# A two-layer graph network on one core: finishing the last row tile bank by bank, with an early test and a branch hint

## The chip, the cores and the metric

The kernel runs on one NeuronCore of a Trainium2 chip. The metric is the device time of one execution in microseconds (us), the median of several runs; smaller is better. A core has five engines that run their own instruction streams and wait for one another by semaphores: PE (TensorE, matrix products, with a separate row PEld for its weight loads), DVE (VectorE), ACT (ScalarE), POOL (GpSimd) and SP (SyncE, which issues DMAs here). Products land in PSUM[...].

A profile is one execution recorded by the hardware. Its span runs from the first to the last instruction and is a little shorter than the measured time.

## The reference, cut to what matters

Two layers, each with a layer norm, a ReLU and a residual. The first attends within graphs of rows; the second is a graph attention over an adjacency matrix of 4096 by 4096 with eight heads of 64 columns.

```python
h = jnp.maximum(_layernorm(x, axis=-1), 0.0)
x = x + _L0_gnn_ref(h, adj, adj, ptr, Wq, bq, Wk, bk, Wv, bv)
h = jnp.maximum(_layernorm(x, axis=-1), 0.0)
x = x + _L1_gnn_ref(h, adj, W, a_origin, a_dst)

def _L1_gnn_ref(x, adj, W, a_origin, a_dst):
    mx = jnp.einsum('nf,hfd->hnd', x, W)
    s_i = jnp.einsum('hnd,hd->hn', mx, a_origin)
    t_j = jnp.einsum('hnd,hd->hn', mx, a_dst)
    logits = s_i[:, :, None] + t_j[:, None, :]
    masked = jnp.where(adj[None] > 0, logits, neg_inf)
    attn = jax.nn.softmax(masked, axis=-1)
    out_h = jnp.einsum('hij,hjd->hid', attn, mx)
    return jnp.transpose(out_h, (1, 0, 2)).reshape(N, H * D)
```

In the softmax of the second layer s_i is constant along a row and drops out. So each row's result is a sum over its neighbours of exp(t_j) times mx_j, divided by the sum of exp(t_j): a product of the 0/1 mask with a matrix of 512 weighted columns and eight columns of weights, and a division.

## The kernel before

The kernel has a straight path, fully unrolled, which holds where the graphs are the row tiles and all sums stay within bounds, and a general path behind a branch, which recomputes everything and is skipped when the bounds hold. It is skipped with the inputs measured here.

The last stage of the straight path, the aggregation, goes over 32 row tiles of 128 rows. Each weighted column is kept as a high and a low part, so a tile is 3 groups (CB) of 174 columns (CW1), each with its low parts behind it: 348 columns a matmul. The last group ends with the sums of weights (columns 512 to 519).

```python
def aggregate(sb, ps_g, i, part):
    mw = sb.tile([P, P // B, N // BY // (P // B)], F32, name="mw", bufs=1)
    ...                                             # four DMAs of the packed mask, a transpose
    at = sb.tile([P, NT, P], F32R, name="at")
    nc.vector.tensor_copy(...)                      # L277: mask bytes to fp32r
    pg = ps_g.tile([P, CB, 512], F32, name="pg")    # three banks
    for j in range(NT):
        for c in range(CB):
            nc.tensor.matmul(                       # L283
                pg[:, c, : 2 * CW1], at[:, j, :],
                part(j)[:, c].rearrange("p s w -> p (s w)"),
                start=(j == 0), stop=(j == NT - 1),
            )
    tot = sb.tile([P, EW], F32, name="tot")
    tot3 = tot.rearrange("p (c w) -> p c w", c=CB)
    nc.scalar.copy(tot3, pg[:, :, :CW1])            # L290
    nc.vector.tensor_tensor(tot3, tot3, pg[:, :, CW1 : 2 * CW1], ALU.add)   # L291
    return tot
```

The loop over the tiles, and the test behind it:

```python
ps_g = straight.enter_context(tc.tile_pool(name="ps_g3", bufs=2, space=PSUM))
...
for i in range(NT):
    row = sb3.tile([P, D], F32, name="row3", bufs=1)
    nc.sync.dma_start(row, x1_d[i])
    tot = aggregate(sb3, ps_g, i, lambda j: parts[j])
    if i + 1 < NT:
        nc.gpsimd.tensor_copy(den_all[:, i : i + 1], tot[:, ES : ES + 1])
    else:
        nc.vector.tensor_scalar(held[:, 5:6], tot[:, ES : ES + 1], 0.0, None, ALU.is_gt)   # L597
    r = small.tile([P, H], F32, name="r")
    nc.vector.tensor_scalar(r, tot[:, ES:EC], 1e-30, None, ALU.max)     # L599
    nc.vector.reciprocal(r, r)                                          # L600
    num = tot[:, :D]
    if i + 1 < NT:
        scaled(num, r)                                                  # L296
        nc.gpsimd.tensor_add(num, num, row)                             # L604
        nc.scalar.dma_start(out[ts(i, P), :], num)
    else:
        for g in range(2):
            half = ts(g, HW)
            scaled(num[:, half], r[:, ts(g, H // 2)])
            nc.vector.tensor_add(num[:, half], num[:, half], row[:, half])   # L610
            nc.scalar.dma_start(out[ts(i, P), half], num[:, half])           # L611
    ...                                             # bounds of earlier stages into held
with tc.tile_pool(name="ps_ok", bufs=1, space=PSUM) as ps:
    all_held = small.tile([P, 1], F32, name="all_held")
    nc.vector.tensor_reduce(all_held, held, AX.X, ALU.min)              # L623
    pt = ps.tile([P, P], F32, name="pt_ok")
    nc.tensor.transpose(pt[:1, :], all_held, ident)                     # L625
    least = small.tile([1, 1], F32, name="least")
    nc.vector.tensor_reduce(least, pt[:1, :], AX.X, ALU.min)            # L627
    nc.vector.tensor_scalar(bad_i, least, 1.0, None, ALU.is_lt)         # L628
bad = nc.values_load(bad_i[0:1, 0:1], min_val=0, max_val=1)             # L629: each engine reads it

with tc.If(bad > 0):                                                    # L632
    ...                                             # the general path, some 270 lines
```

Instructions, semaphores and buffers are ordered and placed by the compiler from the data dependencies; the order on one engine can differ from the program's.

## Time and profile before

| what | value |
|---|---|
| time, median of 3 runs | 974.26 us (972.87 to 974.94) |
| span of the profile | 970.5 us, granted clock 0.992 |
| PE busy | 940.3 us, 97% of the span |
| aggregation matmuls (L283) | 3072, busy 489.6 us |
| DVE busy | 459.4 us, 47% |
| ACT busy | 260.7 us, 27% |
| instruction packets | 41 on queue 8, 31 on queue 14 |

In the profile a line such as "L283 PE MATMUL pg<-part,at ..." names the program's line, the engine, the operation and the tiles written and read. The first number after the bar is the time in which at least one of them ran, the second the mean length of one in ns. The chain of waits is followed back from the last computing instruction, so what comes after that one isn't in it. An engine name with a q is that engine's sequencer, which handles loads of registers, branches and semaphores; these do not count as busy. Instruction packets are the DMA transfers that bring program code to the engines.

### The profile page before, as it was taken

To read this page: it belongs to the slowest core of one execution; us is meant where nothing else is said; L and a number is where in the kernel's file an instruction comes from. 1 tells how busy PE (TensorE), PEld (TensorE's weight loads), DVE (VectorE), ACT (ScalarE), POOL (GpSimd) and SP (SyncE) were. 2 spreads that over 40 slices of the span, in tenths; PEclk is the share of its full clock that TensorE was granted. 3 is DMA by queue.
4 is the path that set the end of the run, shared out by engine and by line. 5 is a ranking of instruction groups with operands and counts; after the bars stand their busy time and mean duration, and the time that the engine had idled before them with its cause. 6 is when DMAs were issued, how large, how long until landed. Compare 5 with 4: busy or idle time off the path is not lost.

```text
span 970.5 us, 13180 instructions
## 1 busy us (share of the span) xinstructions
PE 940.3 (97%) x5051; PEld 817.5 (84%) x5051; DVE 459.4 (47%) x978; ACT 260.7 (27%) x505; POOL 184.0 (19%) x344
## 2 busy tenths in 40 slices
PE   8999999989999998999999999999999999999995
PEld 5676677766677776788999999999999999999994
DVE  4678777866766358655133242433424233242321
ACT  5865666665762222233100000000000000000000
POOL 2211113231122125555110110101011010110100
PEclk9999999999999999999999999999999999999998
DMA  9989889898883033221022312223131221312201
GB/s 343 419 346 378 322 329 364 355 369 317 336 339 148 33 104 108 72 66 55 1 76 56 88 50 82 62 69 87 44 87 52 80 85 47 87 49 82 61 27 37
DMA packets 58042, 148.28 MB, mean 153 GB/s; under 512 B 6386, under 2 KB 23026, under 8 KB 49778
## 3 DMA queue, kind: packets, MB, share of 16 engines
q1 hardware_dynamic: 48178, 130.31, 38.3%
q10 hardware_dynamic: 9792, 17.05, 4.6%
q8 instruction: 41, 0.67, 0.3%
q14 instruction: 31, 0.25, 0.1%
HBM read 113.77 MB, written 33.55 MB: 152 GB/s over the span
## 4 chain that ended last, share of the span: by engine, by line
PE 89%; DVE 3%; DMA 2%; POOL 2%; ACT 2%; issue 1%; SPq 0%; ACTq 0%; DVEq 0%; POOLq 0%
PE pg L283 50%; PE pp L420 11%; PE pp L408 10%; PE pp L243 9%; PE pp L493 3%; PE pss L466 3%; PE pt L127 2%; DMA row<-x_d 1%; POOL part L231 1%; DMA xg<-x 1%; DVE a L136 1%; ACT junk L443 1%; DVE row L121 0%; DVE stats L114 0%; POOL rstd L120 0%
## 5 line engine op out<-in xcount | busy, mean ns | idle before, releaser
L283 PE MATMUL pg<-part,at 128*128 128x348 f32 x3072 | 489.6, 321 | 1.2 <-DVE e L252 1.2
L283 PEld LDWEIGHTS pg<-part,at 128*128 128x128 f32 x3072 | 489.4, 188 | 1.5 <-issue 1.5
L277 DVE CAST at<-at 128x4096 fp32r<-128x4096 fp8e4 x32 | 74.0, 2313 | 312.2 <-PE pg L283 312.2
L290 ACT COPY tot<-pg 128x522 f32<-128x522 f32 x32 | 19.2, 599 | 470.5 <-PE pg L283 470.5
L443 ACT ACTIVATE junk<-a 128x2048 bf16<-128x2048 f32 (+15 forms) x92 | 124.4, 1352 | 48.7 <-DVE x L495 28.0
L243 PE MATMUL pp<-w1x,hT 128*128 128x256 f32 (+1 forms) x512 | 118.4, 385 | 0.0
L420 PE MATMUL pp<-wv,hT 128*128 128x512 f32 x256 | 116.6, 600 | 0.0
L408 PE MATMUL pp<-hT,m_sb 128*128 128x256 f32 x512 | 113.2, 379 | 0.0
L243 PEld LDWEIGHTS pp<-w1x,hT 128*128 128x128 f32 x512 | 95.7, 192 | 13.6
L408 PEld LDWEIGHTS pp<-hT,m_sb 128*128 128x128 f32 x512 | 96.1, 190 | 12.9 <-issue 0.5
L420 PEld LDWEIGHTS pp<-wv,hT 128*128 128x128 f32 x256 | 49.1, 192 | 61.9 <-issue 61.9
L136 DVE TENSOR_SCALAR a<-a 128x512 fp8e4<-128x512 f32 x256 | 98.2, 460 | 0.5 <-DMA a_d<-a 0.4
L595 POOL COPY den_all<-tot 128x1 f32<-128x1 f32 x31 | 5.8, 186 | 369.1 <-DVE tot L291 369.1
L128 ACT ACTIVATE hT<-pt 128x512 f32<-128x512 f32 x64 | 37.0, 598 | 68.8 <-PE pt L127 68.7
L604 POOL TENSOR_TENSOR tot<-tot,row 128x512 f32<-128x512 f32 x31 | 40.0, 1290 | 61.7 <-DVE tot L296 61.7
L231 POOL TENSOR_TENSOR part<-e,part 128x522 fp32r<-128x522 f32 x32 | 42.1, 1316 | 43.0 <-ACT part L230 38.8
L118 POOL TENSOR_SCALAR ve<-mv 128x1 f32<-128x1 f32 x64 | 18.7, 295 | 150.9 <-DVE mv L116 150.8
L252 DVE TENSOR_TENSOR e<-pp,e 128x256 f32<-128x256 f32 x64 | 26.6, 417 | 28.9 <-ACT e L371 25.2
L270 DVE STREAM_TRANSPOSE at<-mw 128x1024 f32<-128x1024 f32 x32 | 39.5, 1236 | 0.0
L120 POOL TENSOR_TENSOR rstd<-ve,neghalf 128x1 f32<-128x1 f32 x64 | 38.5, 604 | 4.4
L424 DVE TENSOR_TENSOR v<-pp,bv_sb 128x512 f32<-128x512 f32 x32 | 22.0, 688 | 36.0 <-PE pp L420 36.0
L412 ACT ACTIVATE gT<-pp,c_sb 128x256 f32<-128x256 f32 x64 | 29.7, 468 | 29.4 <-PE pp L408 29.3
(93 smaller groups left out, 584.1 us busy)
## 6 DMA issues: line engine op xcount, KB each, us to landing
a<-adj SPq DMA_DIRECT2D x64, 1024.0 KB, 13.1
a_d<-a SPq DMA_DIRECT2D x32, 512.0 KB, 10.6
row<-x_d SPq DMA_DIRECT2D x64, 256.0 KB, 3.5
mw<-a_d SPq DMA_DIRECT2D x128, 128.0 KB, 4.0
xg<-x SPq DMA_DIRECT2D x16, 512.0 KB, 4.7
x_d<-x ACTq DMA_DIRECT2D x32, 256.0 KB, 4.2
out<-tot ACTq DMA_DIRECT2D x31, 256.0 KB, 3.8
wkT_sb<-wkT SPq DMA_DIRECT2D x4, 256.0 KB, 6.3
```

The source lines that it names most:

```text
L120: nc.gpsimd.tensor_tensor(rstd, ve, neghalf, ALU.pow)
L128: nc.scalar.activation(dst, pt, AF.Relu)
L136: nc.vector.tensor_scalar(a8v[:, u], av[:, u], 0.0, None, ALU.is_gt, saturate=False)
L231: nc.gpsimd.tensor_sub(dst[:, :, 1, :], e3, dst[:, :, 0, :].bitcast(F32))
L243: nc.tensor.matmul(pm[g][:, :n], hT[:, k, :], w1x[:, k, g * HW : g * HW + n], start=(k == 0), stop=(k == KC - 1),)
L270: nc.vector.transpose(at8.rearrange("p c n b -> p (c n b)").bitcast(F32).rearrange("p (c u n) -> p c u n", c=NW, n=B), mw.rearrange("p u ( ...
L277: nc.vector.tensor_copy(at.rearrange("p (c b) q -> p c b q", b=BY), at8.rearrange("p c q b -> p c b q"))
L283: nc.tensor.matmul(pg[:, c, : 2 * CW1], at[:, j, :], part(j)[:, c].rearrange("p s w -> p (s w)"), start=(j == 0), stop=(j == NT - 1),)
L408: nc.tensor.matmul(pp[:, : G * P], m_sb[:, k, ts(m, P)], hT[:, k, :], start=(k == 0), stop=(k == KC - 1),)
L420: nc.tensor.matmul(pp, hT[:, k, ts(t, P)], wv[:, k, :], start=(k == 0), stop=(k == KC - 1))
L443: nc.scalar.activation(junk[:, c0:c1], a[:, c0:c1], AF.Exp, scale=2.0 * NEG, accum_out=sums[:, n : n + 1],)
L604: nc.gpsimd.tensor_add(num, num, row)
```

## The change

The first 31 tiles are aggregated as before. The last one is finished bank by bank. Its matmuls run group after group in place of alternating: first the last group, which holds the sums of weights, then columns 0 to 173, then 174 to 347. Each group is evacuated, scaled, added to the residual and stored by itself while PE works on the next, so that only the last group's work lies behind the last matmul. The reciprocals of the sums are spread to 512 columns once, as `rb`. The test of the bounds is made from the first group's sums: the minimum over rows is transposed on PE between the second and the third group, so that the flag is known early. Ahead of the last tile a branch hint is placed on all five engines, which tells them that the jump over the general path is likely.

```diff
-    def aggregate(sb, ps_g, i, part):
+    def load_mask(sb, i):
...
+        return at
+
+    def product(pg, at, part, j, c):
+
+        nc.tensor.matmul(
+            pg[:, : 2 * CW1], at[:, j, :], part(j)[:, c].rearrange("p s w -> p (s w)"),
+            start=(j == 0), stop=(j == NT - 1),
+        )
...
-        for i in range(NT):
+        for i in range(NT - 1):
...                                  # the loop's body, without its cases for the last tile
+        tc.mark_branch_hint_location("general", "LikelyTaken", tuple(getattr(mybir.EngineType, e) for e in ("PE", "DVE", "Activation", "Pool", "SP")))
+        i = NT - 1
+        row = sb3.tile([P, D], F32, name="row3", bufs=1)
+        nc.sync.dma_start(row, x1_d[i])
+        at = load_mask(sb3, i)
+        ps_l = straight.enter_context(tc.tile_pool(name="ps_l3", bufs=2, space=PSUM))
+        tot = sb3.tile([P, EW], F32, name="tot")
+        rb = sb3.tile([P, EW], F32, name="tot")
+        for c in (CB - 1, 0, 1):
+            if c == 1:
+                pg = ps_g.tile([P, CB, 512], F32, name="pg")[:, 0]
+            else:
+                pg = ps_l.tile([P, 512], F32, name="pl")
+            for j in range(NT):
+                product(pg, at, lambda j: parts[j], j, c)
+            part = tot[:, ts(c, CW1)]
+            nc.scalar.copy(part, pg[:, :CW1])
+            nc.vector.tensor_tensor(part, part, pg[:, CW1 : 2 * CW1], ALU.add)
+            if c == CB - 1:
+                r = heads_rest(tot)
+                nc.vector.tensor_scalar(held[:, 5:6], tot[:, ES : ES + 1], 0.0, None, ALU.is_gt)
+                all_held = small.tile([P, 1], F32, name="all_held")
+                nc.vector.tensor_reduce(all_held, held, AX.X, ALU.min)
+                nc.vector.tensor_copy(
+                    rb[:, :D].rearrange("p (h d) -> p h d", d=HD),
+                    r[:, :, None].to_broadcast([P, H, HD]),
+                )
+            if c == 0:
+                pt = ps_g.tile([P, CB, 512], F32, name="pg")[:, 0, :P]
+                nc.tensor.transpose(pt[:1, :], all_held, ident)
+                least = small.tile([1, 1], F32, name="least")
+                nc.vector.tensor_reduce(least, pt[:1, :], AX.X, ALU.min)
+                nc.vector.tensor_scalar(bad_i, least, 1.0, None, ALU.is_lt)
+            here = slice(c * CW1, min((c + 1) * CW1, D))
+            nc.vector.tensor_tensor(tot[:, here], tot[:, here], rb[:, here], ALU.mult)
+            nc.vector.tensor_tensor(tot[:, here], tot[:, here], row[:, here], ALU.add)
+            nc.scalar.dma_start(out[ts(i, P), here], tot[:, here])
     bad = nc.values_load(bad_i[0:1, 0:1], min_val=0, max_val=1)

-    with tc.If(bad > 0):
+    with tc.If(bad > 0, label="general"):
```

## The prediction

> **What bounds the kernel now.** I read the page's chain first: 50% of the span is the aggregation matmul and 89% is TensorE. The change leaves all those matmuls in place, so whatever it brings must come from after the last of them. The chain of waits over the last 12 us, then:

> ```profile
> 955.97 2.40 PE pg L283 x15
> 958.37 0.02 issue
> 958.40 0.60 ACT tot L290
> 959.00 0.02 issue
> 959.02 0.71 DVE tot L291
> ...
> 960.60 0.42 DVE tot L296
> 961.02 0.67 DVE tot L610 x2
> 961.69 0.20 DVE least L627
> 961.89 0.02 issue
> 961.91 0.14 DVE bad_i L628
> ```

> Columns are start, length and what ran. TensorE is done at 958.37, and 3.7 us of a serial tail follow: evacuation of three banks, their sum, scaling, residual, the test. But the chain stops at 962.06 and the span at 970.5. The windows view of what lies between (columns: length, busy PE, PEld, DVE, ACT, POOL, clock, DMA share, GB/s):

> ```profile
> 958.40:962.10 3.70, 0.27 (x1) 0.08 (x1) 2.93 (x11) 0.59 (x1) 0.00 (x0) 1.00 0.00 0
> 962.10:962.80 0.70, 0.00 (x0) 0.00 (x0) 0.00 (x0) 0.00 (x0) 0.00 (x0) 0.72 0.62 212
> 962.80:966.10 3.30, 0.00 (x0) 0.00 (x0) 0.00 (x0) 0.00 (x0) 0.00 (x0) 0.50 0.17 49
> ```

> From 962.1 on no engine computes anything; that is 8.4 us, over twice the tail. The instructions of the branch's line, by engine, tell why:

> ```profile
> L632 DVEq EVENT_SEMAPHORE  x2: 21/21/21, 966.1 to 966.2; - x2
> L632 ACTq EVENT_SEMAPHORE  x2: 17/17/17, 966.2 to 966.2; - x2
> L632 PEldq EVENT_SEMAPHORE  x2: 51/51/51, 967.1 to 967.3; - x2
> ...
> L632 DVEq COMPARE_BRANCH  x1: 76/76/76, 962.7 to 962.7; - x1
> L632 PEldq COMPARE_BRANCH  x1: 4322/4322/4322, 962.8 to 962.8; - x1
> L632 ACTq COMPARE_BRANCH  x1: 54/54/54, 962.8 to 962.8; - x1
> ```

> Every engine branches at 962.7 to 963.0, and the next instruction of DVE and ACT comes at 966.1 to 966.2, 3.3 us later; PE's branch itself lasts 4.32 us. The DMA view of 963.6 to 964.6 holds these packets and nothing else:

> ```profile
> q14 instruction: 4, 0.03, 12.8%
> q8 instruction: 1, 0.02, 12.1%
> ```

> Five instruction fetches, one for each engine: the jump goes to code that isn't there yet. A second hole follows. Of the closing line's waits SyncE does three by 967.38 and the next at 969.33, though all they wait for had happened by 967.35 (PE's second semaphore above). Another four 8 KB instruction packets moved at 966.7 to 966.9, so I take that for a second fetch[...]: 1.9 us. The end is then 1.15 us of remaining waits and barrier.

> [...]

> **The change, part by part.**

> *Order of matmuls.* 96 matmuls of 348 columns stay 96, each with its own weight load before and after. The tile now takes 15.30 us (943.1 to 958.4), 159 ns each. Banks are now filled in 32 matmuls, 5.10 us: sums at 948.2, columns 0 to 173 at 953.3, columns 174 to 347 at 958.4. Does accumulating into one bank without rotation slow a matmul? The projections already do so four in a row at 216 ns for 256 columns, no sign of a stall. I assume 159 ns unchanged. The transpose for the test now lies between the second and the third bank: one slot at the 109 ns at which the kernel's other transposes follow one another. Last matmul: 958.36 + 0.11 = 958.47.

> *First two banks and the test.* After the first bank: copy, add, maximum and reciprocal, test, minimum, and a 512-wide copy of the reciprocals, some 2.5 us from 948.2. The copy writes the buffer of the tile before, whose store was issued at 947.24 and lands in 3.8 us, at 951.0; so the scaled sums are out by about 952.5. all_held is ready by 951.7, before the transpose at 953.3. least and bad_i end at about 954.1. Nothing of this delays PE.

> *The third bank, serial.* Lengths from the trace at two sizes. ACT copies: 256 columns 364 ns, 522 columns 599, so 174 columns 364 - 82 x 0.883 = 0.29 us. DVE: 256 columns 420, 512 columns 692, so 174 columns 0.33. Handovers 0.03 each.
> 958.47 + 0.04 + 0.29 (copy) + 0.03 + 0.33 (add) + 0.03 + 0.33 (scale) + 0.03 + 0.33 (residual) + 0.03 = 959.91, issue of the last store, where it was 961.82. It lands 1.7 us later (the median of the two half stores): 961.6, was 963.5. Gain to here: 1.9 us.

> *The flag is early.* PE, POOL and SP have nothing after the flag but their own work: SP and POOL can read it at 954.2 (0.57 us) and branch at 954.9; PE branches after its last matmul, about 958.6. Even unhinted, their fetches end at 958.2 and 962.9. DVE reads it at 959.9 and branches at 960.6. ACT reads it after its last store issue (0.36): 960.3 + 0.47 + 0.1 = 960.9.

> *The hint.* It is put ahead of the last tile, some 15 us before the branch; the fetch needs 3.3. If it works, ACT goes on at about 961.2 in place of 960.9 + 3.3 = 964.2. I take 0.3 us for a hinted jump, a guess of a few branch lengths (50 to 76 ns); no run shows it yet. SyncE's second fetch is hidden with or without the hint, since SyncE then sits at the target from 958.2 at the latest, and its next block (3.0 us after arrival in this trace, 966.3 to 969.3) is there by 961.2.

> *Sum.* What ends last is SyncE, waiting for the last store at 961.6. Then eight resets (0.6; the store's semaphore, next in rotation, is probably an early one in its list), nine closing waits at 0.07 (0.63), drains (0.13), and the barrier as now, 969.73 to 970.47 (0.74): 963.7. The span falls from 970.5 to 963.7, by 6.8 us, 1.9 of it from the shorter tail, 3.0 from the jump, 1.9 from SyncE's second fetch. On the 974.26 us measured: 967.5.

> **The rivals.**
> *The hint does nothing, or is lost.* [...] Then ACT and DVE are the last: ACT at 964.2, two resets and a drain 0.25, SyncE's last waits 0.35, drains and barrier 0.87: 965.7. Gain 4.8, time 969.5. I give this 25%.
> *Nothing in the tail counts, the stores' landing ends the kernel anyway.* The trace speaks against: the last store's packets end at 963.4, 7 us before the end.
> *Single-bank accumulation is slower.* At 10 ns more for each of 96 matmuls it takes back 1.0 us: 968.5. The 216 ns row speaks against it; it could as well be a little faster[...].
> *A wait takes its place.* The order on an engine isn't the program's: at 927.81 DVE casts the mask of the last tile before it adds tile 29's banks at 930.02, though the program has two tiles' work between. The hint stands ahead of the last tile's mask in the program. If nothing may pass it, the cast (2.29 us) falls behind tile 30's add, 944.5, and PE, which is through with tile 30 at 943.1, waits some 3.7 us: 971.4. If on the contrary the hint floats far ahead[...]: 970 and more. Likewise a transpose moved behind the third bank makes the flag 0.7 us late and opens all five fetches again: 970. I give these together 15%. The banks speak for no wait: six for the rotating pair, two for the new pool, all long free.
> [...]

> **Range and chances.** 967.5 is the sum with a working hint; the rivals nearly all lie above it, up to 972, and pull the middle to 967.9. The runs of before themselves spread by 2.1 us. Eight times in ten: 965.0 to 971.5. Two per cent would be 19.5 us, more than all that follows the last matmul (12.1), so faster by over 2% is about 1%; slower by over 2% needs a stall no part here explains, 1%.

> **What would show it.** Right: the last store issued near 959.9; compare-branches of SP and POOL before 956 and of ACT near 961; ACT's next instruction within 0.5 us of its branch, with its instruction packets near 944 and none after the branch; no hole in SyncE's closing waits; span near 963.7. Wrong: 3.3 us after ACT's or DVE's branch (hint lost), a last matmul later than 959 (accumulation, transpose, or a cast held back by the hint), a bad_i after the last matmul (order).

## The result, and the profile after

| | before | after |
|---|---|---|
| time, median of 6 runs each | 973.04 us (972.23 to 974.94) | 966.17 us (962.86 to 967.85) |
| ratio after to before | | 0.9924, 95% interval 0.9906 to 0.9942 |
| span of the profile | 970.5 us | 961.1 us |
| last aggregation matmul ends at | 958.36 | 955.31 |
| from there to the end of the span, "tail" below | 12.11 us | 5.76 us |

The two profiles' spans differ by 9.4 us, the medians by 6.9. Some 3.1 us of the 9.4 are not the change's: the aggregation starts at 468.7 us in the profile before and at 465.6 in the one after, and over all profiles at 465.6 to 470.1, whatever the kernel. From there to its last matmul it takes 489.6 us before and 489.7 after, the slot of the transpose. All else that the change brings lies behind the last matmul, so the tail is what is compared from here on. It fell by 6.35 us, or 6.25 less the slot.

The chain of waits of the changed kernel from the last tile on (start, length, what ran):

```profile
939.93 10.20 PE pl L284 x64
950.13 0.11 PE pg L655
950.24 5.09 PE pg L284 x32
955.33 0.02 issue
955.35 0.31 ACT tot L642
955.66 0.02 issue
955.69 0.35 DVE tot L643
956.03 0.02 issue
956.06 0.35 DVE tot L660
956.41 0.02 issue
956.43 0.34 DVE tot L661
```

The first two groups of the last tile take 10.20 us for 64 matmuls, the third 5.09 for 32: 159 ns each, as with alternating banks. The transpose takes a slot of 0.11 us. Behind the last matmul four short operations are left, 1.46 us, where 3.7 us of them stood before. The windows view of the tail (length, busy PE, PEld, DVE, ACT, POOL, clock, DMA share, GB/s), cut at the issue of the last store and at its landing:

```profile
955.31:956.80 1.49, 0.00 (x1) 0.00 (x0) 1.02 (x3) 0.30 (x1) 0.00 (x0) 1.00 0.00 0
956.80:959.18 2.38, 0.00 (x0) 0.00 (x0) 0.00 (x0) 0.00 (x0) 0.00 (x0) 0.96 0.15 44
959.18:961.10 1.92, 0.00 (x0) 0.00 (x0) 0.00 (x0) 0.00 (x0) 0.00 (x0) 0.50 0.00 0
```

So the tail is now 1.5 us of work, 2.4 us of a store that lands, 1.9 us of closing waits and barrier. The branch's line, by the sequencer of each engine (count, then shortest, median and longest in ns, then the first and last start):

```profile
L666 SPq EVENT_SEMAPHORE  x9: 17/17/17, 952.3 to 959.7; - x9
...
L666 PEldq EVENT_SEMAPHORE  x2: 51/51/51, 955.4 to 955.6; - x2
L666 DVEq EVENT_SEMAPHORE  x2: 21/21/21, 957.7 to 957.8; - x2
L666 ACTq EVENT_SEMAPHORE  x2: 17/17/17, 958.2 to 958.3; - x2
L666 POOLq COMPARE_BRANCH  x1: 65/65/65, 951.5 to 951.5; - x1
L666 SPq COMPARE_BRANCH  x1: 70/70/70, 951.8 to 951.8; - x1
L666 PEldq COMPARE_BRANCH  x1: 408/408/408, 952.9 to 952.9; - x1
L666 DVEq COMPARE_BRANCH  x1: 89/89/89, 957.1 to 957.1; - x1
L666 ACTq COMPARE_BRANCH  x1: 68/68/68, 957.7 to 957.7; - x1
```

PE's branch lasts 408 ns where it lasted 4322, DVE and ACT go on about 0.5 us after theirs where it was 3.3. SyncE branches 3.5 us before the last matmul ends, does its first reset at 952.3 and then waits for the store until 959.18. Where the hint itself stands is the surprise. The closing line of the program, to which the compiler books it:

```profile
L939 POOLq BRANCH_PREFETCH_HINT  x1: 48/48/48, 0.7 to 0.7; - x1
...
L939 PEldq BRANCH_PREFETCH_HINT  x1: 50/50/50, 0.8 to 0.8; - x1
```

It was written ahead of the last tile, but stands at the head of all five streams, some 950 us before the branch. That it depends on no other instruction, so that the compiler could move it there, is my reading.

### The profile page after: what moved, and what is told of

It reads as the page before. It is cut to its first block, busy times and chain, and to the rows that moved or that the text cites. A ratio compares the mean times of both kernels' runs of the same rounds, so it can differ in the third digit from the quotient of the medians. Undisturbed runs are those within 1.5% of the kernel's fastest.

```text
span 961.1 us, 13194 instructions
## 1 busy us (share of the span) xinstructions
PE 937.3 (98%) x5051; PEld 817.2 (85%) x5051; DVE 460.7 (48%) x983; ACT 260.7 (27%) x507; POOL 185.0 (19%) x344
## 4 chain that ended last, share of the span: by engine, by line
PE 89%; DVE 4%; DMA 2%; POOL 2%; ACT 2%; issue 1%; SPq 0%; ACTq 0%; DVEq 0%; POOLq 0%
PE pg L284 50%; PE pp L428 11%; PE pp L416 10%; PE pp L243 9%; PE pp L501 3%; PE pss L474 3%; PE pt L127 2%; DMA row<-x_d 1%; PE pl L284 1%; POOL part L231 1%; DMA xg<-x 1%; DVE a L136 1%; DVE row L121 1%; ACT junk L451 1%; POOL rstd L120 0%
## 5 line engine op out<-in xcount | busy, mean ns | idle before, releaser
L284 PE MATMUL pg<-part,at 128*128 128x348 f32 x3008 | 479.6, 322 | 1.2 <-DVE e L252 1.2
L284 PEld LDWEIGHTS pg<-part,at 128*128 128x128 f32 x3008 | 479.1, 188 | 1.6 <-issue 1.5
L416 PEld LDWEIGHTS pp<-hT,m_sb 128*128 128x128 f32 x512 | 96.2, 190 | 12.8 <-issue 0.5
```

Source lines behind the costliest of these rows:

```text
L284: nc.tensor.matmul(pg[:, : 2 * CW1], at[:, j, :], part(j)[:, c].rearrange("p s w -> p (s w)"), start=(j == 0), stop=(j == NT - 1),)
L416: nc.tensor.matmul(pp[:, : G * P], m_sb[:, k, ts(m, P)], hT[:, k, :], start=(k == 0), stop=(k == KC - 1),)
```

## The experiments

All tails in one table; the sections follow. "Landing" is from the issue of the last store to its last semaphore update; all numbers are us.

| kernel | tail | jump of ACT | landing | hole in SyncE's waits |
|---|---|---|---|---|
| before | 12.11 | 3.31 | 1.76 | 1.9 |
| after (three profiles) | 5.76, 5.75, 5.79 | 0.42 | 2.37, 2.36, 2.39 | none |
| before with the hint | 7.16 | 0.42 | 1.77 | none |
| after without the hint | 6.58 | 2.89 | 2.46 | 0.4, before ACT arrives |
| after, test behind the third bank | 6.56 | 0.42 | 3.17 | none |
| after, hint on DVE and ACT alone | 6.08 | 0.42 | 2.69 | none |
| before, one spare load on SyncE | 11.85 | 3.16 | 1.77 | 1.7 |
| before, hint on POOL alone | 10.09 | 3.14 | 1.77 | none |
| after, two more DVE products at the end | 6.01 | 0.42 | 2.61 | none |
| after, order 2, 1, 0, three stores | 5.13 | 0.42 | 1.73 | none |
| after, order 2, 1, 0, two stores | 4.48, 4.48 | 0.42 | 1.60, 1.60 | none |

### The changed kernel again

No edit.

> The changed kernel once more, for how far its end repeats. Tail means the time from the end of the last aggregation matmul to the end of the span: 12.1 us before, 5.8 us after. Theory: the tail is a fixed chain and repeats within 0.2 us; the last store lands 2.4 us after its issue because its rows are 696 B. Rival: the 2.4 us (1.7 for the half stores of before) were chance; then the store lands in 1.7 us and the tail is about 5.1 us.

Measured: tail 5.75 us, landing 2.36. The tail repeats to a few hundredths (a third profile, further down: 5.79), and the long landing is no chance. So single profiles of a variant can be compared by their tails, though their times can't to that accuracy.

### The hint alone

```diff
         for i in range(NT):
+            if i + 1 == NT:
+                tc.mark_branch_hint_location("general", "LikelyTaken", ...)   # all five engines
             row = sb3.tile([P, D], F32, name="row3", bufs=1)
...
-    with tc.If(bad > 0):
+    with tc.If(bad > 0, label="general"):
```

> The kernel before with the hint alone. Theory (a hint given at any distance works, the compiler puts it at the program's start, some 960 us ahead): every engine's next instruction 0.4 to 0.5 us after its branch in place of 3.3, PE's branch 0.4 in place of 4.3, no instruction packets between the branches and the first instruction at the target; SyncE's second fetch (3.0 us from its arrival) stays, since nothing else has become earlier: tail 12.1 - 2.9 = 9.2 us, time about 3 us less than before. Rival (the hint is lost over 960 us, the short jump of the changed kernel comes from something else): tail 12.1 us, time as before.

Measured: tail 7.16 us, 967.28 us, ratio to before 0.9952 (0.9924 to 0.998). The branch's line of this kernel:

```profile
L634 SPq EVENT_SEMAPHORE  x9: 17/17/17, 963.5 to 964.1; - x9
...
L634 ACTq EVENT_SEMAPHORE  x2: 17/17/17, 963.3 to 963.3; - x2
L634 DVEq EVENT_SEMAPHORE  x2: 21/21/21, 963.3 to 963.4; - x2
...
L634 PEldq COMPARE_BRANCH  x1: 408/408/408, 962.7 to 962.7; - x1
L634 ACTq COMPARE_BRANCH  x1: 68/68/68, 962.8 to 962.8; - x1
L634 SPq COMPARE_BRANCH  x1: 70/70/70, 963.0 to 963.0; - x1
```

The branches come at the same times as before, and all engines go on 0.4 to 0.5 us later in place of 3.3. The hint works from the head of the program; the rival falls. But the tail is 2.0 us shorter than the theory said: SyncE's second stall is gone too, which I had not expected of the hint. Instruction packets still move at 963.8 to 964.1, but SyncE goes through its waits (964.2 to 965.4 with the barrier) without stopping for one. It gets its own test further down. The one line of the hint alone is thus worth 4.95 of the change's 6.35 us.

### The change without the hint

```diff
-        tc.mark_branch_hint_location("general", "LikelyTaken", ...)
```

> The changed kernel without the hint. Theory (the hint spares the fetch at each jump, but only the engines that branch last, DVE and ACT, are on the path): 3.3 us behind each branch, SP's, POOL's and PE's of it hidden under the third bank's matmuls; ACT goes on 6 us after the last matmul, tail 7.2 us, 1.5 us more than with the hint. Rival A (the early flag alone makes all jumps harmless): tail 5.8 us. Rival B (the hint is worth a whole fetch, 3.3 us): tail 9 us.

Measured: tail 6.58 us, 966.68 us, ratio 0.9952 (0.9924 to 0.9979). The branch's line:

```profile
L665 SPq EVENT_SEMAPHORE  x9: 17/17/17, 956.8 to 962.3; - x9
...
L665 PEldq EVENT_SEMAPHORE  x2: 51/51/51, 958.9 to 959.0; - x2
L665 DVEq EVENT_SEMAPHORE  x2: 21/21/21, 962.4 to 962.5; - x2
L665 ACTq EVENT_SEMAPHORE  x2: 17/17/17, 963.1 to 963.2; - x2
...
L665 PEldq COMPARE_BRANCH  x1: 3442/3442/3442, 955.4 to 955.4; - x1
L665 DVEq COMPARE_BRANCH  x1: 76/76/76, 959.5 to 959.5; - x1
L665 ACTq COMPARE_BRANCH  x1: 54/54/54, 960.2 to 960.2; - x1
```

The last matmul of this profile ends at 957.78. Every engine stands behind its jump again, 2.5 to 3.0 us and 3.44 in PE's branch, but SyncE and PE go on at 956.8 and 958.9, and DVE and ACT alone (962.4 and 963.1) behind the store's landing (961.7). ACT's jump took 2.89 us, not 3.3, which is 0.4 of the 0.6 us by which the tail is below what was expected. SyncE has a short hole in its closing waits, 0.4 us (962.60 to 962.96) where it was 1.9, and had reached the target nearly 6 us before; it then waits for ACT until 963.27, which sets the end. Both rivals fall: the early flag doesn't make the jumps harmless, and the hint is not worth a whole jump's 3.3 us on top of it. It is worth 0.8 us.

### The test behind the third bank

```diff
-            if c == 0:
+            if c == 1:
                 pt = ps_g.tile([P, CB, 512], F32, name="pg")[:, 0, :P]
```

> The changed kernel with the test of the bounds behind the third bank, as before, and with the hint. Theory (the early flag is worth SyncE's second fetch, which needs 3.0 us from its arrival at the target): SyncE arrives some 3.4 us after the last matmul, has its next block at 6.4, tail about 7.5 us. Rival (with the hint the early flag is worth nothing, since the last store's landing ends last): tail about 5.9 us.

Measured: tail 6.56 us, 966.84 us. The number lies between the two and the reason is neither. SyncE reaches the target 2.15 us after the last matmul, earlier than I had reckoned, and has no hole. What is longer is the last store:

```profile
L662 ACTq DMA_DIRECT2D out<-tot x3: 339/339/339, 951.7 to 959.2; - x3
...
DMA to landing us min/median/max: 1.6/1.7/3.2
```

The store of the second bank now lands in 1.6 us (2.1 to 2.6 in the profiles with the early test), the last one in 3.2. The instruction fetches behind the jumps of POOL, SyncE and PE moved from the one to the other: they lie 2.7 to 1.3 us before the end of the matmuls with the early test and 2.5 to 2.7 us after it with the late one. The times of single packets in the trace show the stores held up: each store has 144 packets, 128 rows and 16 small ones (under 512 B), as many as its semaphore has updates. With the early test the second store's last ones start 1.6 to 2.0 us after its issue, and one of its 16 semaphore updates comes late and alone; with the late test they have all started by 1.24 us. The last store's packets start until 2.6 us after its issue here, until 1.26 us in the changed kernel. That a fetch holds up packets is only seen, not tested by itself, and it is not the whole of the long landing, as a run further down shows.

With the hint, then, the early test brings 0.8 us, all of it in that landing. That divides the change: in the order hint, bank by bank, early test, the tails are 12.11, 7.16, 6.56 and 5.76 us, so the parts bring 4.95, 0.60 and 0.80. Finishing bank by bank brings so little because the last store, issued 2.0 us earlier (1.49 us after the last matmul in place of 3.46), takes 1.4 us longer to land.

### The hint on the two engines that branch last

```diff
-("PE", "DVE", "Activation", "Pool", "SP")
+("DVE", "Activation")
```

> The changed kernel with the hint on DVE and ACT alone. Theory (SP, POOL and PE branch 2.4 to 3.8 us before the last matmul ends, so their fetches are hidden): 2.5 to 3.4 us behind the branches of SP, POOL and PE, 0.4 to 0.5 behind DVE's and ACT's, tail as with all five hints, 5.6 to 6.0 us. Rival (SyncE's own hint is what removes its second fetch from the path): SyncE has a hole in its closing waits again and the tail is above 6.3 us.

Measured: 2.6 and 2.8 us behind the branches of POOL and SP, PE's branch 3.74 us, 0.4 to 0.5 us for DVE and ACT; tail 6.08 us. That is a little over the range expected. All of the 0.3 us over the full hint is in the landing, 2.69 in place of 2.37: 1.3 us after the last store's issue 135 of its 144 packets have moved, with a 16 KB instruction packet among them, where all 144 have in the changed kernel. So the jumps of the three early engines are hidden without the hint, but in this one profile the landing with their later packet beside it is 0.3 us longer. SyncE, unhinted here, had no hole either, which spoke against the rival and asked for the next two runs.

### What made SyncE's hole, and what removed it

The hole of the kernel before, in the waits of its closing line, read in two windows:

```profile
L905 SPq EVENT_SEMAPHORE  x3: 28/28/203, 967.0 to 967.2; - x3
```

```profile
L905 SPq EVENT_SEMAPHORE  x5: 27/28/28, 969.3 to 969.6; - x5
```

First, one more instruction on SyncE's queue, without a hint:

```diff
     nc.scalar.dma_start(bk_sb, bk)
+    spare = const.tile([P, KC], F32, name="spare")
+    nc.sync.dma_start(spare, bk)
```

> The kernel before, unhinted, with one more small DMA on SyncE's queue at the start, which moves all that follows in SyncE's instructions by one. Theory L (SyncE's hole of 1.9 us in the kernel before is a matter of where the jump's target lies[...]; the hint, being one more instruction, moved it): the hole is gone, SyncE runs from its first reset to its last wait without a stop, tail 10.1 us. Theory H (the hint itself brings in more code): the hole stays, at most one instruction earlier, tail 12.1 us.

```profile
L907 SPq EVENT_SEMAPHORE  x2: 28/28/28, 966.7 to 966.8; - x2
```

```profile
L907 SPq EVENT_SEMAPHORE  x6: 27/28/28, 968.6 to 968.9; - x6
```

Two waits stand before the hole in place of three: it sits at a fixed place of the code, and moves by one with one more instruction. But it doesn't vanish (tail 11.85 us), so a shift by the hint's own slot isn't what removed it. Theory L falls as it was put. Then the hint on an engine that is never the last:

```diff
-("PE", "DVE", "Activation", "Pool", "SP")        # of the kernel before with the hint
+("Pool",)
```

> The kernel before with the hint on POOL alone, an engine that never ends last. Theory P (with any hint the code at the jump's target is placed anew for all engines, and that is what removed SyncE's hole of 1.9 us, also in the run in which SyncE had no hint): 3.3 us stay behind the branches of DVE, ACT, SP and 4.3 of PE, POOL's is 0.4, and SyncE runs through its waits without a hole: tail about 10.1 us. Theory H (an engine's own hint removes its own second fetch): the hole stays, tail about 12.1 us.

The same closing line of this kernel, and its branches:

```profile
L907 SPq EVENT_SEMAPHORE  x8: 28/28/65, 967.5 to 968.0; - x8
```

```profile
L634 SPq EVENT_SEMAPHORE  x9: 17/17/17, 966.8 to 967.5; - x9
L634 POOLq EVENT_SEMAPHORE  x2: 17/17/17, 963.6 to 963.7; - x2
...
L634 POOLq COMPARE_BRANCH  x1: 65/65/65, 963.1 to 963.1; - x1
...
L634 SPq COMPARE_BRANCH  x1: 45/45/45, 963.4 to 963.4; - x1
```

SyncE still pays 3.4 us for its jump (963.4 to 966.8), and then does nine resets and eight waits without a stop. Tail 10.09 us, 2.0 below the kernel before. POOL's own jump, 0.4 us, is of no use there: POOL goes on at 963.6, and SyncE does its closing waits from 967.5 to 968.0. So a hint on POOL alone removes the hole on SyncE, whose own jump is as slow as ever. The label on the branch, which comes with the hint, is not what does it: the changed kernel without the hint keeps the label and has its 0.4 us hole behind the second wait, where the run with the spare load has its own. That the code at the target is laid out anew where a hint names it is my inference from these runs; the profile shows no addresses.

### The last store

After the changes the landing is the largest piece of the tail. Two theories on its 2.4 us. First, later fetches:

```diff
             nc.scalar.dma_start(out[ts(i, P), here], tot[:, here])
+            if c == 1:
+                for _ in range(2):
+                    nc.vector.tensor_tensor(rb[:, :D], tot[:, :D], rb[:, :D], ALU.mult)
```

> The changed kernel with two DVE products of 512 columns into the spent buffer rb behind the last sum, so that DVE jumps some 1.1 us later (its results are not used). Theory C (the last store lands 2.4 us after issue in place of 1.7 because the instruction fetches behind DVE's and ACT's jumps, 8 KB each, share the DMA engines with it): DVE's fetch falls behind the landing, the store lands in at most 1.9 us, tail about 5.2 us in spite of the longer DVE work. Rival S (696-byte rows take longer than 1024-byte ones): landing 2.4 us, tail 5.8 us or more.

Measured: DVE's jump 1.1 us later, no instruction packet until 3.79 us after the last matmul, landing 2.61 us (4.10 after it), tail 6.01. The first of these packets moves 2.30 us after the store's issue. By then 15 of the store's 16 semaphore updates have come, 11 of them later than 1.8 us, without any fetch beside them; only the last one, at 2.61 us, has a fetch beside it. So theory C, which had 1.9 us at most, falls for this store. Rival S fell with the next two runs, whose last store has rows of 696 bytes too and lands in 1.60 and 1.73 us. They change the order of the groups, so that the last store writes columns 0 to 173; one of them also joins the first two stores:

```diff
-        for c in (CB - 1, 0, 1):
+        for c in (CB - 1, 1, 0):
-            if c == 1:
+            if c == 0:
                 pg = ps_g.tile([P, CB, 512], F32, name="pg")[:, 0]
...
-            if c == 0:
+            if c == 1:
                 pt = ps_g.tile([P, CB, 512], F32, name="pg")[:, 0, :P]
...                                     # in the two-store version alone:
-            nc.scalar.dma_start(out[ts(i, P), here], tot[:, here])
+            if c == 1:
+                here = slice(CW1, D)
+            if c < CB - 1:
+                nc.scalar.dma_start(out[ts(i, P), here], tot[:, here])
```

> The changed kernel with groups in the order 2, 1, 0 and two stores in place of three (columns 174 to 511 after the second group, 0 to 173 after the third). Theory (behind the landing SyncE still has to do the resets that stand after the store's semaphore in its list, at 0.07 us each; with two stores the last one has the last semaphore of the list and none is left): landing to end 1.3 to 1.4 us in place of 1.9, tail about 5.2 us if the landing takes 2.4 us as before. Rival (the resets are done while SyncE waits): tail as before, 5.76 us.

> The changed kernel with the groups in the order 2, 1, 0 and the three stores kept; the last one writes columns 0 to 173 in place of 174 to 347. Theory (in the two-store run two things were gained: 0.6 us by the store's place in SyncE's list, 0.75 us by the columns that the last store writes): the last store lands 1.6 us after issue, the resets behind it stay, tail about 5.0 us. Rival (the shorter landing came with the smaller number of stores): landing 2.4 us, tail 5.7 us.

Measured: tail 4.48 us with two stores, 5.13 with three. The theory of the two-store run had 5.2, with a landing of 2.4 us; the quick landing is what it had not foreseen. The windows of the two-store version, cut as above:

```profile
957.77:959.26 1.49, 0.01 (x1) 0.00 (x0) 1.02 (x3) 0.30 (x1) 0.00 (x0) 1.00 0.00 0
959.26:960.87 1.61, 0.00 (x0) 0.00 (x0) 0.00 (x0) 0.00 (x0) 0.00 (x0) 1.00 0.19 60
960.87:962.30 1.43, 0.00 (x0) 0.00 (x0) 0.00 (x0) 0.00 (x0) 0.00 (x0) 0.76 0.02 6
```

The work is the same 1.49 us. The landing is 1.6 in place of 2.4, with two stores or three: it goes with the columns written last. Behind the landing stand 1.4 us in place of 1.9: the last of two stores has semaphore 108, the last in SyncE's list, so the resets before it are done while the store flies and one is left (at 960.9, landing 960.87); the third store had come round to 100, the first of the DMA semaphores in that list, and eight resets follow its landing (959.19 to 959.70). So each gain of the two-store version shows in a pair of runs.

The changed kernel's DMA view from 956.0 to 958.2 (packets, MB, share of the DMA engines) tells where the long landing lies:

```profile
q10 hardware_dynamic: 144, 0.09, 13.4%
```

All 144 packets of the last store have moved by 958.2, and it lands at 959.18. They start by 1.26 us after the issue, those of the quick store of the two-store version by 1.24. What is later is the semaphore: its 16 updates come at 1.50 to 2.37 us after the issue, those of the quick store at 1.43 to 1.60. The place at the end does not seem to be what does it: in the three-store run of the order 2, 1, 0, columns 174 to 347 are the second store, and 6 of its 16 updates come later than 1.75 us, where columns 0 to 173 in that place have one in the changed kernel. Why columns 174 to 347 land later than 0 to 173, both of 128 rows of 696 bytes, no run tells. In seven profiles they took 2.4 to 3.2 us as the last store; columns 0 to 173 took 1.6 to 1.7 in three.

> The two-store version once more, timed, beside the changed kernel in the same job: tail 4.5 us again, time 1.3 us below the changed kernel's and about 8 us below the kernel before. Rival (4.5 us was chance, the landing varies): tail 5.2 us.

> The changed kernel, timed in the same job as the two-store version: tail 5.75 us, time about 6.4 us below the kernel before.

| timed | median | ratio to before | tail |
|---|---|---|---|
| before | 973.34 us | | |
| changed kernel | 965.87 us | 0.993 (0.9907 to 0.9953) | 5.79 |
| two stores, order 2, 1, 0 | 964.95 us | 0.9914 (0.9891 to 0.9937) | 4.48 |

The two-store version has the shortest tail. Its 0.9 us over the changed kernel, where 1.3 was expected, lies within the scatter of the times; the tails, which repeat to 0.05 us, put it at 1.3. The changed kernel is 7.5 us below the kernel before here, where 6.4 was expected, and the tails give 6.3.

## Why the prediction was right, point by point

The time predicted was 967.9 us (967.5 as the bare sum), the time measured 966.17; 1.2 us of the distance is that the kernel before has 973.04 us over six runs where it had 974.26 over three. The drop was 6.9 us where the sum had 6.8, and that this fits so closely is luck: the 95% interval of the ratio allows 5.6 to 9.1 us, and the tails give 6.25. Counted from the last matmul the sum had 963.7 - 958.47 = 5.23 us, and the profile 5.76. The cause was right: the gain came from the jump, SyncE's second stall and the shorter tail, none of it from the matmuls.

- **Pace and transpose.** 159 ns a matmul and one slot of 0.11 us, both as reckoned. The rival of slower single-bank accumulation is refuted by the 10.20 and 5.09 us of the chain.
- **The test.** bad_i ends 4.4 us before the last matmul does (950.89), as in the sum. The copy of the reciprocals waits for the store of the tile before until 947.72, as foreseen, and PE is not held up by it.
- **The third bank.** Issue of the last store 1.44 us after the last matmul in the sum, 1.49 measured.
- **The flag.** SP and POOL branch 3.5 and 3.8 us before the last matmul ends, 3.6 in the sum; ACT 2.41 us after it, 2.4 in the sum. PE does not branch after its last matmul, as I had written, but 2.4 us before that ends (952.92 and 955.31): its sequencer was that far ahead of the matmuls here. DVE's too reads the flag (956.45) while its last sum still runs (956.43 to 956.77), and branches 1.75 us after the last matmul, 2.1 in the sum.
- **The hint.** 0.3 us a jump guessed, 0.42 to 0.50 measured. Its place was wrong: not 15 us ahead but at the head of the program, and no instruction packet near 944. Nor was there "none after the branch": two 8 KB packets follow DVE's and ACT's jumps, at 958.26 and 959.10, and no engine stops for them: the resets of both run through from 957.7 to 958.3. The rival had named the hint's place ("floats far ahead") and expected harm from it; none showed: the aggregation took 489.7 us, the transpose included, where it had 489.6.
- **The landing.** The term that was off most: 1.7 us taken from the half stores, 2.37 measured. 0.67 too little. The work before the store took 0.05 more than the sum and the closing waits 0.2 less (1.9 for 2.1; they are eight and not nine), which gives the 0.53 us by which the tail exceeds it.
- **The parts of the sum.** Here the step failed, though the total held. I had booked 1.9 us to the shorter tail, 3.0 to the jump, 1.9 to SyncE's second fetch (a fetch by my reading of the packets from 966.7 on), as if each were brought by its own part. The runs give 4.95 us for the hint alone and 5.53 for all the rest without the hint, 10.5 together, of which 6.35 are had: the early flag hides the same waits behind the jumps that the hint shortens from 3.3 us to 0.4. No run has the bank-by-bank finish with neither hint nor early flag, so the 5.53 can't be divided further. On top of all the rest the hint brought 0.8 us, where the prediction's own rival had 2.0 (965.7 without it, 963.7 with it). The 1.9 us for the shorter tail were right for the store's issue, but the landing took back 0.6 of them. And SyncE's second stall is removed by the hint, even by one on another engine, which I had not foreseen; with the early flag and no hint 0.4 us of it is left, ahead of ACT's arrival, as I had foreseen.
- **The rival "hint lost".** It had 7.2 us behind the last matmul; the run without the hint had 6.58, with ACT last, as it said. The wait was shorter: the jumps of POOL, SP, DVE and ACT took 2.5 to 3.0 us there, where the engines fetch at different times, and 3.1 to 3.7 in the runs in which four or five fetch at once. That this is the reason is not tested by itself.
- **Slips in the working.** Two do not bear on the sum: POOL's branch in the kernel before took 45 ns, below the 50 to 76 given; and the held-back cast comes to 971.2 (967.5 + 3.7), not 971.4.

## What to carry to other kernels

Where a chain of waits ends well before the span does, look at what the sequencers do there: a forward jump over code that isn't run cost 3.3 us here, and SyncE's stall behind it 1.9 more, in a kernel whose every engine was idle by then; one line of a hint took back 4.95 us. A flag that decides a jump is worth having early: engines with nothing left to do then fetched beneath the others' work (packets at 952.6 to 954.0, last matmul to 955.31), and the early test was worth 0.8 us here with the hint in place. But hint and early flag paid for the same thing here, and their gains didn't add: 4.95 and 5.53 us alone, 6.35 together. When only microseconds at the end are at stake, compare the stretch from a fixed event (the last matmul) to the end rather than whole times: it repeated to 0.05 us here while times scattered by several.
